# Splitting the left sums of a quad over two pairs and writing ScalarE's order in a fused two-layer graph kernel

## The chip, the cores and the metric

The kernel runs on one core of one Trainium2 chip. A core has TensorE (matrix products into PSUM), VectorE (DVE in the profile), ScalarE (ACT), GpSimd (POOL) and SyncE (SP, which issues transfers), each with an instruction queue of its own, and 16 DMA engines. The metric is the device time of one execution in microseconds; lower is better.

## The reference

There are 128 graphs of 128 nodes with 512 features each, and an adjacency matrix for each graph, all in 32-bit floats. Two residual layers follow each other:

```python
# layer 0
h = maximum(layernorm(x), 0)
Xw = h @ Wv + bv;  sj = Xw @ aw[:d];  si = Xw @ aw[d:]
alpha = adj * exp(leaky_relu(sj[None, :] + si[:, None] + ab, 0.2))
T = alpha / (sum(alpha, -1) + 1e-12)
H = h @ Wk[0] + (T @ h) @ Wk[1] + (T @ T @ h) @ Wk[2] + sum(bk)
x = x + relu(H)
# layer 1
h = maximum(layernorm(x), 0)
q, k = split(h @ Wqk);  v = h @ Wv
w = mask / sqrt(512) * sum(q * (adj @ (k * mask)), -1)
out = x + softmax(w over the nodes) * v
```

## The kernel before

**Tiling.** Two graphs make a pair (64 pairs), two pairs a quad (32 quads). All products of a pair by a weight matrix go through Strassen's scheme: two graphs by two halves of the contraction form a 2x2 block matrix, and seven products on sums of blocks (called 1 to 7) replace eight. The function strassen (L361) writes the products in the order 1, 5, 6, 2, 7, 3, 4 into four PSUM banks a, b, c, e. Between them ScalarE copies partial results from bank to bank or to a buffer: U1, b from a (L378), after product 1; S5, the buffer from e (L380), after product 5; U2, c from b (L382), after product 6; S7, the buffer from c (L386), after product 7. Product 6 adds onto U1, product 7 onto U2, and product 4 adds into c once S7 has read it.

**Layer 0, the loop over pairs (L644).** There are two Strassen rounds in each pass. y10(p) computes h times Wk[1] and Wk[0] in bank set 1 and uses 512 columns; y2(p + 2) computes h times Wk[2] and the attention columns in bank set 2, with 257 columns. One pass p runs, on TensorE: y10(p) with the two transposes of the transition matrix T (t_transposed, L482) after product 2; inner(p) and outer(p), which multiply by the transposed T; y2(p + 2). Around these:
- attention(p) (L453) makes T from the attention columns and the adjacency, on VectorE with one exponential on ScalarE (L463); its last lines multiply the transposed adjacency aT by the mask on ScalarE (L479) and store it for layer 1 (L480).
- outer(p) ends with four drains of the set 1 banks by VectorE (L533), which give the residual x1, and its store.
- seed_a and seed_e (L491, L495) have ScalarE write the bias into banks a and e of set 1 once those are drained; the next y10 adds to it.
- norm2_statistics(p) and norm2(p) (L546, L537) normalise x1 for layer 1: mean and variance on VectorE (L282, L283), a logarithm and an exponential on ScalarE (L287, L288), five small operations on VectorE, two activations over 512 columns on ScalarE (L306). The result is stored in DRAM (h2d) and read back by blocks (hv) for transposing. norm0(p + 3) does the same for the x of a later pair.
- y2's ends: block (0, 0) is copied by ScalarE (Y00, L434) after product 2, block (1, 0) (Y10, L437) after product 4; the other two are VectorE additions.
- prepare (L553) forms weight sums for layer 1 in pairs 3 to 9.

**The left sums of layer 1.** for_layer1(p) (L403), called behind y10(p + 1)'s additions, transposes hv into the tile fw of the pair's quad on VectorE (L412, four transposes of 128x256). The pool of fw has one buffer: `left = layer0.enter_context(tc.tile_pool(name="left", bufs=1))` (L683). In the second pair of a quad, four 128x512 additions and subtractions (L420, L421, L423, L424) complete its eight slots, and two transfers of 1 MB each by GpSimd's queue (L422, L425) store slots 0 to 3 and 4 to 7.

**What sets the order.** The engines run at once; each runs its own instructions in the order in which they stand in its queue. A scheduler decides this order from priorities and dependences. The helper behind (L83) adds to it: an instruction is placed after a named earlier one, `done[what]`. TensorE's order is written out (ordered, L88); on VectorE and ScalarE some places are written and the others are the scheduler's. A new tile in a pool with one buffer is written only when all users of the old tile, transfers among them, are done.

**Layer 1** begins when layer 0's pools are closed (L712). It works quad by quad on the stored sums and doesn't change here.

Of the kernel before, what the change touches and what calls it, by code (L numbers as in the profile page):

```python
# [16 lines left out]
def kernel(  # L17
# [25 lines left out]
    nc = tc.nc  # L43
# [233 lines left out]
    def statistics(src, gate="warm"):  # L277

        mv = small.tile([P, G, 2], FP, name="mv")
        for j in range(G):  # L280
            st = small.tile([P, 6], FP, name="st")
            nc.vector.bn_stats(st, src[:, j, :])  # L282
            nc.vector.bn_aggr(mv[:, j, :], st)  # L283
        mean, var = mv[:, :, 0], mv[:, :, 1]

        r = small.tile([P, 6, G], FP, name="r")
        behind(gate, nc.scalar.activation, r[:, 0], var, AF.Ln, bias=eps)  # L287
        nc.scalar.activation(r[:, 1], r[:, 0], AF.Exp, scale=-0.5)  # L288
        nc.vector.tensor_mul(r[:, 2], r[:, 1], r[:, 1])  # L289
        nc.vector.scalar_tensor_tensor(r[:, 3], var, EPS, r[:, 2], op0=OP.add, op1=OP.mult)  # L290
        nc.vector.tensor_scalar(r[:, 4], r[:, 3], -0.5, 1.5, op0=OP.mult, op1=OP.add)  # L291
        rs = small.tile([P, 2, G], FP, name="rs")
        nc.vector.tensor_mul(rs[:, 0], r[:, 1], r[:, 4])
        done["rs"] = nc.vector.scalar_tensor_tensor(rs[:, 1], mean, -1.0, rs[:, 0], op0=OP.mult, op1=OP.mult).ins  # L294
        return rs

    def norm_relu(src, permuted=False, rs=None):


        rs = statistics(src) if rs is None else rs  # L300
        h = front.tile([P, G, D], FP, name="h")
        for j in range(G):
            to, at = h[:, j, :], src[:, j, :]
            if permuted:
                to, at = unpermuted(to), at.rearrange("p (c f a) -> p c f a", c=DC, f=Q)
            nc.scalar.activation(to, at, AF.Relu, bias=rs[:, 1, j:j + 1], scale=rs[:, 0, j:j + 1])  # L306
        return h

    def unpermuted(h):
# [48 lines left out]
        return dict(zip((5, 6, 7, 3, 1, 2, 4), [s[:, i] for i in range(4)] +  # L358
                        [blocks[0, 0], blocks[0, 1], blocks[1, 1]]))

    def strassen(banks, left, right, s, first, ends, steps={}, gate="warm"):  # L361

        w = right[1].shape[2:]
        a, b, c, e = (t[:, :w[0]] if len(w) == 1 else t for t in banks)

        def product(bank, i, start=False):
            if len(w) > 1:
                bank = bank.rearrange("p (k o) -> p k o", k=w[0])  # L370
            for k in range(HC):
                ordered(nc.tensor.matmul, bank, left[i][:, k * P:(k + 1) * P], right[i][:, k],
                        start=(start and k == 0), stop=(k == HC - 1), skip_group_check=True)
            if i in steps:
                steps[i]()

        product(a, 1, first)
        nc.scalar.copy(b, a)  # L378
        product(e, 5, first)
        done["s"] = behind(gate, nc.scalar.copy, s[:, 0], e).ins  # L380
        product(b, 6)
        done["u2"] = behind("s", nc.scalar.copy, c, b).ins  # L382
        product(a, 2)
        ends[0, 0](a)
        product(c, 7)
        done["s7"] = nc.scalar.copy(s[:, 1], c).ins  # L386
        ends[1, 1](e, s[:, 1])
        product(b, 3)
        ends[0, 1](b, s[:, 0])
        product(c, 4)  # L390
        ends[1, 0](c)
# [6 lines left out]
    def begin(p):  # L398
        hT = lefts.tile([P, G, DC, N], FP, name="x")
        transposed(HV.pop(p), hT)  # L400
        LEFT[p] = left_sums(hT)

    def for_layer1(p):  # L403

        q, second = divmod(p, 2)
        if not second:
            FW[q] = left.tile([P, 8, G, HC, N], FP, name="fw")
        f = FW[q]
        blocks, hv = f[:, L21:SLOT[4] + 1] if second else f[:, 0:SLOT[2] + 1:2], HV2.pop(p)
        for j in range(G):  # L410
            for k in range(2):
                nc.vector.transpose(blocks[:, k, j].rearrange("p f (n b) -> p f n b", n=Q),  # L412
                                    hv[:, j].rearrange("p n (k f a) -> p k f n a", k=2, f=HC)[:, k])
        if second:
            fv = FW.pop(q).rearrange("p o j k n -> p o (j k n)")
            fd = FD[q].rearrange("p o j k n -> p o (j k n)")
            at = {o: fv[:, i] for o, i in SLOT.items()}

            queue = nc.gpsimd if q + 1 < NQ else nc.sync
            nc.vector.tensor_add(at[5], fv[:, L21], at[4])  # L420
            nc.vector.tensor_sub(at[6], at[5], at[1])  # L421
            queue.dma_start(fd[:, :4].rearrange("p o n -> p (o n)"), fv[:, :4].rearrange("p o n -> p (o n)"))  # L422
            nc.vector.tensor_sub(at[7], at[1], fv[:, L21])  # L423
            done["c12"] = nc.vector.tensor_sub(at[3], at[2], at[6]).ins  # L424
            queue.dma_start(fd[:, 4:].rearrange("p o n -> p (o n)"), fv[:, 4:].rearrange("p o n -> p (o n)"))  # L425

    def y2(p, steps={}, gate=None):


        add = partial(behind, gate, nc.vector.tensor_add) if gate else nc.vector.tensor_add  # L430
        y = Y2[p] = front.tile([P, G, 2, WP], FP, name="y2")[:, :, :, :W2]
        s = front.tile([P, 2, WP * 2], FP, name="s", bufs=1)[:, :, :W2]
        strassen(set2, LEFT[p], right2, s, True, {
            (0, 0): lambda a: nc.scalar.copy(y[:, 0, 0], a),  # L434
            (1, 1): lambda e, t: add(y[:, 1, 1], e, t),
            (0, 1): lambda b, t: add(y[:, 0, 1], b, t),
            (1, 0): lambda c: nc.scalar.copy(y[:, 1, 0], c)}, steps)  # L437
        if p > 1:

            t = small.tile([P, G, S32], FP, name="pzt", bufs=1)  # L440
            behind(gate, nc.vector.transpose, t, y[:, :, 0, :S32])
            d = dram.tile([G, Q, S32], FP, name="pzd")
            nc.gpsimd.dma_start(d.rearrange("g q b -> q g b"), t[::S32])  # L443
            PZ[p] = front.tile([P, G, N], FP, name="pz")
            nc.gpsimd.dma_start(PZ[p].rearrange("p g n -> p (g n)"), bcast(d, 0, G * N))
        else:
            PZ[p] = a2[:, :G * N].rearrange("p (g n) -> p g n", g=G)
# [5 lines left out]
    def attention(p, early_work=None):  # L453

        a, y, pz = ag.pop(p), Y2[p], PZ.pop(p)
        z = front.tile([P, G, N], FP, name="z", bufs=1)
        for j in range(G):
            done["pz"] = nc.vector.tensor_scalar(z[:, j, :], pz[:, j, :], y[:, j, 1, HD:], cz,
                                                 op0=OP.add, op1=OP.add).ins
        if early_work:  # L460
            behind("pz", early_work)
        behind("left" if early_work else "pz", nc.vector.scalar_tensor_tensor, z, z, 0.2, z, op0=OP.mult, op1=OP.max)
        done["z"] = nc.scalar.activation(z, z, AF.Exp).ins  # L463
        d = small.tile([P, 2, G], FP, name="d")
        for j in range(G):
            nc.vector.scalar_tensor_tensor(z[:, j, :], z[:, j, :], 1.0, a[:, j, :], op0=OP.mult,
                                           op1=OP.mult, accum_out=d[:, 0, j:j + 1])
        nc.vector.tensor_scalar(d[:, 0], d[:, 0], 1e-12, None, op0=OP.add)
        nc.vector.reciprocal(d[:, 1], d[:, 0])
        t = T[p] = front.tile([P, G, N], FP, name="t", bufs=1)  # L470
        for j in range(G):
            done["t"] = nc.vector.tensor_scalar(t[:, j, :], z[:, j, :], d[:, 1, j:j + 1], None,
                                                op0=OP.mult).ins
        aT = front.tile([P, G, N], FP, name="aT", bufs=1)
        nc.vector.transpose(aT.rearrange("p g n -> p (g n)"),  # L475
                            agb.pop(p).rearrange("p g q i -> p (g q i)"))
        for j in range(G):
            b = p * G + j
            behind("z", nc.scalar.activation, aT[:, j, :], aT[:, j, :], AF.Copy, scale=maskT[:, b:b + 1])  # L479
        nc.sync.dma_start(ATD[p], aT)  # L480

    def t_transposed(p):  # L482
# [54 lines left out]
    def norm2(p):  # L537

        if p not in RS2:
            norm2_statistics(p)  # L540
        rs = RS2.pop(p)
        HV2[p] = by_blocks(behind("s7", norm_relu, X1[p], rs=rs), H2D[p])

    RS2 = {}

# [93 lines left out]
    with tc.issue_after(done["hv"]):  # L639
        load_x(3)  # L640
        load_adj(2)
        rows(rl[:, :, 1], wv1)

    for p in range(NP):  # L644
        def between():
            if p == 0:
# [3 lines left out]
            if p + 2 < NP:  # L650
                behind("t", begin, p + 2)
            if p + 3 < NP:
                behind("left", norm0, p + 3)
            if p == 2:
                rightl.update(behind("rs", combine, {(kh, k): rl[:, kh * HC:(kh + 1) * HC, k]
                                                     for kh in range(2) for k in range(2)},
# [3 lines left out]

        if p > 1:
            behind("rs2", attention, p)
        y10(p, {1: between, 2: lambda: t_transposed(p)})
        if p > 0:
            behind("c12", for_layer1, p - 1)
        if p == NP - 2:
# [19 lines left out]
        if p + 2 < NP:  # L686
            y2(p + 2, {2: partial(norm2_statistics, p)}, "rs2")
        if p + 1 < NP:
            seed_a()
            seed_e()  # L690
        norm2(p)
        if p + 3 < NP:
            load_adj(p + 3)
# [416 lines left out]
```

## Time and profile before

| quantity | value |
|---|---|
| median of 3 runs | 2290.12 us (2287.68 to 2291.49) |
| the profiled execution's own time | 2288.12 us |
| its span, first to last instruction | 2286.3 us |
| TensorE, matmuls | busy 2235.6 us, 98% |
| VectorE / ScalarE / GpSimd | busy 1629.4 / 1273.6 / 700.6 us |
| DMA | 507.78 MB, mean 222 GB/s |
| layer 0 within the span | about 0 to 1480 us; one pair 21.8 to 22.8 us in the steady part |
| PE clock over the span | 0.995 of full speed |

A line of the timeline reads: start and duration in us, engine, source line, operation, output <- inputs, shapes, and in brackets the idle time of the engine before it and what ended it. Line L91 is the helper of all ordered matmuls and L86 that of everything placed by behind, so the tiles tell what an instruction is: `c<-w,x` is product 4 of y2, `c<-t,x` product 4 of y10, or product 7 where it has `sx`. A line of the waits reads: who waited for whom, us in total, times, the longest. The times are of one execution.

### The profile page before, as it was taken

To read this page: it belongs to the slowest core of one execution; us is meant where nothing else is said; L and a number is where in the kernel's file an instruction comes from. 1 tells how busy PE (TensorE), PEld (TensorE's weight loads), DVE (VectorE), ACT (ScalarE), POOL (GpSimd) and SP (SyncE) were. 2 spreads that over 40 slices of the span, in tenths; PEclk is the share of its full clock that TensorE was granted. 3 is DMA by queue.
4 is the path that set the end of the run, shared out by engine and by line. 5 is a ranking of instruction groups with operands and counts; after the bars stand their busy time and mean duration, and the time that the engine had idled before them with its cause. 6 is when DMAs were issued, how large, how long until landed. Compare 5 with 4: busy or idle time off the path is not lost.

```text
span 2286.3 us, 28949 instructions
## 1 busy us (share of the span) xinstructions
PE 2235.6 (98%) x8227; PEld 1544.0 (68%) x8227; DVE 1629.4 (71%) x4463; ACT 1273.6 (56%) x2933; POOL 700.6 (31%) x827
## 2 busy tenths in 40 slices
PE   9899999999999999999999999999999999999998
PEld 5565656566665656666565666578888888888886
DVE  5677767777677677767767776567777776776777
ACT  4455545555555555555555555446666666666665
POOL 3011111221212122121211212145455555455554
PEclk9999999999999999999999999999999999999999
DMA  8587787676766767676676666668888888888877
GB/s 232 162 259 224 238 243 238 199 220 205 225 207 198 239 199 220 206 224 203 202 238 200 217 206 216 200 231 237 234 239 234 238 233 229 247 235 224 254 236 195
DMA packets 343503, 507.78 MB, mean 222 GB/s; under 512 B 33178, under 2 KB 198426, under 8 KB 326958
## 3 DMA queue, kind: packets, MB, share of 16 engines
q1 hardware_dynamic: 302060, 382.40, 52.8%
q0 software_dynamic: 40992, 123.00, 20.2%
q8 instruction: 65, 1.06, 0.2%
q14 instruction: 96, 0.79, 0.1%
q10 hardware_dynamic: 290, 0.53, 0.1%
HBM read 289.62 MB, written 216.18 MB: 221 GB/s over the span
## 4 chain that ended last, share of the span: by engine, by line
PE 77%; ACT 4%; DVE 3%; DMA 2%; issue 1%; POOL 0%; SPq 0%; DVEq 0%; POOLq 0%
PE a L91 23%; PE b L91 21%; PE c L91 21%; PE e L91 13%; ACT h L306 2%; DMA rw<-rwd 1%; DMA h2d<-h 1%; DMA hv<-h2d 0%; ACT b L378 0%; DMA pwd<-pwt 0%; ACT r L288 0%; ACT y L437 0%; DMA pw<-pwd 0%; ACT r L86 0%; DVE r L291 0%
## 5 line engine op out<-in xcount | busy, mean ns | idle before, releaser
L111 POOL DMA_DIRECT2D agb<-in_adj_dram x256 | 150.5, 592 | 524.1 <-DVE aT L475 490.6
L570 POOL TENSOR_TENSOR c<-s,c 128x512 f32<-128x512 f32 (+1 forms) x186 | 199.9, 1089 | 259.6 <-DVE s L570 254.8
L91 PE MATMUL a<-r,x 128*128 128x512 f32 x512 | 241.6, 594 | 4.9 <-ACT a L493 4.8
L91 PE MATMUL b<-rw,in 128*128 128x256 f32 x896 | 216.4, 381 | 0.0
L289 DVE TENSOR_TENSOR r<-r 128x2 f32<-128x2 f32 x128 | 20.6, 161 | 235.4 <-ACT r L288 235.3
L91 PEld LDWEIGHTS b<-rw,in 128*128 128x128 f32 x896 | 171.3, 191 | 23.6
L91 PEld LDWEIGHTS a<-r,x 128*128 128x128 f32 x512 | 97.0, 190 | 101.0 <-issue 92.1
L570 POOL TENSOR_TENSOR c<-c 128x1024 f32<-128x1024 f32 (+1 forms) x70 | 152.4, 2186 | 13.5 <-DVE c L570 13.2
L91 PE MATMUL a<-w,x 128*128 128x257 f32 x512 | 131.9, 380 | 2.0 <-DVE x L338 2.0
L91 PE MATMUL b<-w,sx 128*128 128x257 f32 x512 | 132.1, 380 | 0.3 <-ACT b L378 0.3
L91 PE MATMUL b<-t,sx 128*128 128x512 f32 x256 | 122.2, 599 | 8.3 <-ACT b L378 8.2
L91 PE MATMUL c<-t,x 128*128 128x512 f32 x256 | 121.2, 596 | 4.8 <-ACT s L386 4.8
L378 ACT COPY b<-a 128x257 f32<-128x257 f32 (+1 forms) x128 | 59.4, 464 | 117.6 <-PE a L91 116.0
L443 POOL DMA_DIRECT2D pzd<-pzt x62 | 37.0, 596 | 281.2 <-DVE pzt L86 275.8
L91 PE MATMUL e<-t,sx 128*128 128x512 f32 x256 | 121.3, 596 | 0.0
L306 ACT ACTIVATE h<-xg,rs 128x512 f32<-128x512 f32 x128 | 97.2, 807 | 43.2 <-DVE rs L294 42.2
L91 PE MATMUL c<-t,sx 128*128 128x512 f32 x256 | 120.5, 593 | 0.0
L570 ACT ACTIVATE c<-c,wcol 128x512 f32<-128x512 f32 x125 | 87.1, 719 | 59.7 <-DVE wcol L570 58.7
L91 PE MATMUL b<-r,sx 128*128 128x512 f32 x256 | 120.3, 592 | 0.0
L570 DVE SCALAR_TENSOR_TENSOR junk<-agg,wscale,c 128x512 f32<-128x512 f32 x128 | 97.9, 765 | 31.3 <-POOL c L570 26.0
L422 POOL DMA_DIRECT2D fd<-fw x31 | 17.4, 561 | 310.2 <-DVE fw L421 297.6
L91 PE MATMUL c<-rw,in 128*128 128x256 f32 x448 | 108.5, 382 | 2.8 <-ACT c L570 2.8
(248 smaller groups left out, 5332.4 us busy)
## 6 DMA issues: line engine op xcount, KB each, us to landing
fd<-fw POOLq DMA_DIRECT2D x62, 1024.0 KB, 6.9
x1d<-x SPq DMA_DIRECT2D x64, 512.0 KB, 3.4
h2d<-h SPq DMA_DIRECT2D x64, 512.0 KB, 2.9
hv<-h2d SPq DMA_DIRECT2D x256, 128.0 KB, 4.2
f<-fd SPq DMA_DIRECT2D x32, 1024.0 KB, 6.3
xg<-in_x_dram SPq DMA_DIRECT2D x63, 512.0 KB, 4.6
hd<-h SPq DMA_DIRECT2D x63, 512.0 KB, 2.8
hv<-hd SPq DMA_DIRECT2D x252, 128.0 KB, 3.1
```

What stands on the lines that cost most here:

```text
L91: done["mm"] = op(*args, **how).ins
L111: nc.gpsimd.dma_start(agb[p][c * S32:(c + 1) * S32].rearrange("p g q i -> p (g q) i"), v[c])
L289: nc.vector.tensor_mul(r[:, 2], r[:, 1], r[:, 1])
L306: nc.scalar.activation(to, at, AF.Relu, bias=rs[:, 1, j:j + 1], scale=rs[:, 0, j:j + 1])
L378: nc.scalar.copy(b, a)
L422: queue.dma_start(fd[:, :4].rearrange("p o n -> p (o n)"), fv[:, :4].rearrange("p o n -> p (o n)"))
L443: nc.gpsimd.dma_start(d.rearrange("g q b -> q g b"), t[::S32])
L570: done[engine] = op(*args, **how).ins
```

## The change

Four things change; no product, sum, copy or activation is added or removed, and the same bytes are moved.
- The four left sums of a quad are split: slots 5 and 6 (at[5], at[6]) are formed in the second pair of the quad, as before, and the first half is stored. The other two sums and the second half's store (`upper`) are put off until for_layer1 is called for the first pair of the next quad, just ahead of the request for the new fw tile.
- In y2, Y00 is placed behind the exponential of the second norm's statistics, and S7 behind Y00. The second norm's logarithm stays behind U2.
- The two seeds are placed behind S7 of y2; norm0(p + 3)'s activations behind S7 of y10, while its statistics stay where they were.
- U1 of y10 is placed behind the activations of the second norm, and the mask's multiplications with their store behind U1 (from pair 2 on).

```diff
-        nc.scalar.activation(r[:, 1], r[:, 0], AF.Exp, scale=-0.5)
+        done["ln"] = nc.scalar.activation(r[:, 1], r[:, 0], AF.Exp, scale=-0.5).ins
...
-    def strassen(banks, left, right, s, first, ends, steps={}, gate="warm"):
+    def strassen(banks, left, right, s, first, ends, steps={}, gate="warm", seventh="warm"):
...
-        nc.scalar.copy(b, a)
+        done["ba"] = behind("warm" if first or "h2" not in done else "h2", nc.scalar.copy, b, a).ins
...
-        done["s7"] = nc.scalar.copy(s[:, 1], c).ins
+        done["s7"] = behind(seventh, nc.scalar.copy, s[:, 1], c).ins
...
     def for_layer1(p):
         q, second = divmod(p, 2)
         if not second:
+            if q:
+                SUMS.pop(q - 1)()
             FW[q] = left.tile([P, 8, G, HC, N], FP, name="fw")
...
+            def upper():
+                behind("c12", nc.vector.tensor_sub, at[7], at[1], fv[:, L21])
+                done["c12"] = nc.vector.tensor_sub(at[3], at[2], at[6]).ins
+                store_half(1)
             nc.vector.tensor_add(at[5], fv[:, L21], at[4])
-            nc.vector.tensor_sub(at[6], at[5], at[1])
-            queue.dma_start(fd[:, :4].rearrange("p o n -> p (o n)"), fv[:, :4].rearrange("p o n -> p (o n)"))
-            nc.vector.tensor_sub(at[7], at[1], fv[:, L21])
-            done["c12"] = nc.vector.tensor_sub(at[3], at[2], at[6]).ins
-            queue.dma_start(fd[:, 4:].rearrange("p o n -> p (o n)"), fv[:, 4:].rearrange("p o n -> p (o n)"))
+            done["c12"] = nc.vector.tensor_sub(at[6], at[5], at[1]).ins
+            store_half(0)
+            SUMS[q] = upper
+            if q + 1 == NQ:
+                SUMS.pop(q)()
...
+        def y00(a):
+            done["y00"] = behind("ln" if gate else "warm", nc.scalar.copy, y[:, 0, 0], a).ins
...
-            (0, 0): lambda a: nc.scalar.copy(y[:, 0, 0], a),
+            (0, 0): y00,
...
-            behind("z", nc.scalar.activation, aT[:, j, :], aT[:, j, :], AF.Copy, scale=maskT[:, b:b + 1])
+            behind(gate, nc.scalar.activation, aT[:, j, :], aT[:, j, :], AF.Copy, scale=maskT[:, b:b + 1])
...
             if p + 3 < NP:
-                behind("left", norm0, p + 3)
+                RS0[p + 3] = behind("left", statistics, xg[p + 3])
...
+        def norms():
+            if p and p + 3 < NP:
+                behind("s7", norm0, p + 3, RS0.pop(p + 3))
+        steps = {1: between, 2: lambda: t_transposed(p), 3: norms}
+        if p > 1:
+            steps[5] = lambda: masked(p, "ba")
+        y10(p, steps)
...
-            seed_a()
-            seed_e()
+            behind("s7", seed_a)
+            behind("s7", seed_e)
```

More of the change, by code (lines that the diff above doesn't have):

```diff
@@ L305, in norm_relu @@
                 to, at = unpermuted(to), at.rearrange("p (c f a) -> p c f a", c=DC, f=Q)
-            nc.scalar.activation(to, at, AF.Relu, bias=rs[:, 1, j:j + 1], scale=rs[:, 0, j:j + 1])
+            done["h"] = nc.scalar.activation(to, at, AF.Relu, bias=rs[:, 1, j:j + 1], scale=rs[:, 0, j:j + 1]).ins
         return h
@@ L401, in begin @@
         LEFT[p] = left_sums(hT)
+    SUMS = {}
     def for_layer1(p):
@@ L411, in for_layer1 @@
             for k in range(2):
-                nc.vector.transpose(blocks[:, k, j].rearrange("p f (n b) -> p f n b", n=Q),
-                                    hv[:, j].rearrange("p n (k f a) -> p k f n a", k=2, f=HC)[:, k])
+                done["c12"] = nc.vector.transpose(blocks[:, k, j].rearrange("p f (n b) -> p f n b", n=Q),
+                                                  hv[:, j].rearrange("p n (k f a) -> p k f n a", k=2, f=HC)[:, k]).ins
         if second:
@@ L419, in for_layer1, with store_half @@
             queue = nc.gpsimd if q + 1 < NQ else nc.sync
-            nc.vector.tensor_add(at[5], fv[:, L21], at[4])
-            nc.vector.tensor_sub(at[6], at[5], at[1])
-            queue.dma_start(fd[:, :4].rearrange("p o n -> p (o n)"), fv[:, :4].rearrange("p o n -> p (o n)"))
-            nc.vector.tensor_sub(at[7], at[1], fv[:, L21])
-            done["c12"] = nc.vector.tensor_sub(at[3], at[2], at[6]).ins
-            queue.dma_start(fd[:, 4:].rearrange("p o n -> p (o n)"), fv[:, 4:].rearrange("p o n -> p (o n)"))
+            def store_half(i):
+                half = slice(4 * i, 4 * i + 4)
+                queue.dma_start(fd[:, half].rearrange("p o n -> p (o n)"), fv[:, half].rearrange("p o n -> p (o n)"))
+            def upper():
+                behind("c12", nc.vector.tensor_sub, at[7], at[1], fv[:, L21])
+                done["c12"] = nc.vector.tensor_sub(at[3], at[2], at[6]).ins
+                store_half(1)
+            nc.vector.tensor_add(at[5], fv[:, L21], at[4])
+            done["c12"] = nc.vector.tensor_sub(at[6], at[5], at[1]).ins
[3 more added lines that the diff above has]
+                SUMS.pop(q)()
     def y2(p, steps={}, gate=None):
@@ L432, in y2 @@
         s = front.tile([P, 2, WP * 2], FP, name="s", bufs=1)[:, :, :W2]
+        def y00(a):
+            done["y00"] = behind("ln" if gate else "warm", nc.scalar.copy, y[:, 0, 0], a).ins
         strassen(set2, LEFT[p], right2, s, True, {
-            (0, 0): lambda a: nc.scalar.copy(y[:, 0, 0], a),
+            (0, 0): y00,
             (1, 1): lambda e, t: add(y[:, 1, 1], e, t),
             (0, 1): lambda b, t: add(y[:, 0, 1], b, t),
-            (1, 0): lambda c: nc.scalar.copy(y[:, 1, 0], c)}, steps)
+            (1, 0): lambda c: nc.scalar.copy(y[:, 1, 0], c)}, steps, seventh="y00")
         if p > 1:
@@ L476, in attention, with masked @@
                             agb.pop(p).rearrange("p g q i -> p (g q i)"))
+        MASKED[p] = aT
+        if p < G:
+            masked(p, "z")
+    MASKED = {}
+    def masked(p, gate):
+        aT = MASKED.pop(p)
         for j in range(G):
             b = p * G + j
-            behind("z", nc.scalar.activation, aT[:, j, :], aT[:, j, :], AF.Copy, scale=maskT[:, b:b + 1])
+            behind(gate, nc.scalar.activation, aT[:, j, :], aT[:, j, :], AF.Copy, scale=maskT[:, b:b + 1])
         nc.sync.dma_start(ATD[p], aT)
@@ L541, in norm2 @@
         rs = RS2.pop(p)
-        HV2[p] = by_blocks(behind("s7", norm_relu, X1[p], rs=rs), H2D[p])
+        h = behind("s7", norm_relu, X1[p], rs=rs)
+        done["h2"] = done["h"]
+        HV2[p] = by_blocks(h, H2D[p])
     RS2 = {}
@@ L642 @@
         rows(rl[:, :, 1], wv1)
+    RS0 = {}
     for p in range(NP):
@@ L662 @@
             behind("rs2", attention, p)
-        y10(p, {1: between, 2: lambda: t_transposed(p)})
+        def norms():
[5 more added lines that the diff above has]
+        y10(p, steps)
         if p > 0:
```

## The prediction

> **What bounds the kernel now.** I read the page's busy times first.
>
> ```profile
> span 2286.3 us, 28949 instructions
> PE 2235.6 (98%) x8227; PEld 1544.0 (68%) x8227; DVE 1629.4 (71%) x4463; ACT 1273.6 (56%) x2933; POOL 700.6 (31%) x827
> ```
>
> TensorE is idle for only 2286.3 - 2235.6 = 50.7 us, so nothing done on another engine gains more than that. Next, the waits of PE:
>
> ```profile
> PE b L91 <- ACT b L378: 8.5, 18, 0.6
> PE a L91 <- ACT a L493: 4.8, 2, 3.9
> PE c L91 <- ACT s L386: 4.8, 9, 1.1
> ```
>
> Then the timeline of layer 0. Call "turn k" the stretch from the first product of y2(k+2) to that of y2(k+3), with y10(k+1) in it. From one first inner product (`a<-y,tt`) to the next an undisturbed turn takes 21.758 us (721.60 to 743.35). Summed over the 59 intervals of pairs 3 to 61, the excess over 21.758 is 33.4 us, 21.7 of it in the 49 of pairs 13 to 61. There it repeats every six pairs (1.05, 0.73, 0.74, 0, 0, 0.2): ScalarE's copy of U1 (L378) stands behind two normalisations, or the copy of product 7 (L386) does:
>
> ```profile
> 710.63 1.52 ACT L306 ACTIVATE h<-x,rs 128x512 f32<-128x512 f32 x2 [1.02 <-DVE rs L294]
> ...
> 712.06 0.58 ACT L378 COPY b<-a 128x512 f32<-128x512 f32 x1
> ...
> 712.69 1.98 PE L91 MATMUL b<-t,sx 128*128 128x512 f32 x4 [0.48 <-ACT b L378]
> ```
>
> The copy waits for no product: it starts as the second activation leaves.
>
> **The Trainium skill.** "TensorE: Matmul & The Clock Gate", What's actually happening: TensorE's clock halves after an idle window and recovers after a busy one; the 3413 ns windows run freely. The trace agrees: its three single slow stretches begin at 1461.94, 1530.21 and 2274.31 us, whole multiples of 3.4133 apart. Half a window idle can do, though:
>
> ```profile
> core 0: us, PE busy (x) PEld busy (x) DVE busy (x) ACT busy (x) POOL busy (x), PEclk, DMA share, GB/s
> 1458.53:1461.94 3.41, 1.10 (x3) 0.62 (x4) 3.38 (x8) 1.11 (x2) 1.09 (x2) 1.00 0.46 192
> 1461.94:1465.35 3.41, 3.41 (x6) 1.35 (x5) 1.17 (x7) 0.98 (x3) 0.00 (x0) 0.50 0.98 386
> 1526.80:1530.21 3.41, 1.14 (x5) 1.04 (x6) 3.27 (x8) 3.28 (x13) 0.00 (x0) 1.00 0.91 337
> 59.07:62.48 3.41, 1.43 (x7) 0.93 (x6) 1.45 (x4) 0.00 (x0) 0.00 (x0) 1.00 0.47 114
> 62.48:65.89 3.41, 3.36 (x15) 2.73 (x16) 3.34 (x11) 1.23 (x4) 0.00 (x0) 1.00 0.02 5
> ```
>
> With 1.10 or 1.14 us busy in a window the next ran at 0.50; with 1.43 it did not. So 2.27 us idle inside one window cost half of 3.41 = 1.7 us, 1.98 cost nothing. "DMA: Bandwidth & Descriptors", Anatomy of one DMA: a GpSimd-issued transfer takes about 2.0 us plus its bytes at 436 GB/s, since its semaphore waits for the write receipt: 4.4 us for 1 MB, an estimate; the trace has 5.0 (below) and is used. The same clock page, Architectural detail, says VectorE and ScalarE are strict first-in-first-out; in the trace, too, work stands behind a waiting instruction.
>
> **The change part by part.** Zero is the first y2 product (702.54 in the timeline), undisturbed.
>
> ScalarE's orders (built programs, engine by engine): before, they differ from turn to turn; after, all are U1, S5, U2 of y2, logarithm, exponential, Y00, S7, both seeds, h2, Y10, h2, attention exponential, U1 of y10, mask twice, S5, U2, transposed transition, logarithm and exponential of the next norm (about that copy), S7, h0 twice. No arithmetic is added or removed.
> - U1 (L378): product 1 of y10 (at 6.07) ends near 8.0. In front: S7 4.54, seeds 4.81 and 5.3 (0.59 each), h2 5.75 to 6.5, Y10 to 6.8, h2 to 7.55, exponential to 7.95. U1 goes at 8.0, its limit is near 8.9: the 0.48 us waits go.
> - S7 (L386): before the two h0 of 0.76 each: the 0.46 us waits go. If the logarithm in front were late instead: attention exponential 7.55, its row sums, scaling, transposes, sums and statistics 6.1 us (713.05 to 719.18), logarithm 13.7, exponential to 14.2; S7 is due at 15.1. Covered by 0.9.
> - Second norm's logarithm before Y00 and S7: variance at 2.1, U2 done 3.15, Y00 due 3.67. Covered by 1 us in an ordinary turn.
> - Seeds behind S7 end at 5.9, needed at 6.07 by y10: just covered. Masks and their store (L480) slip by under 1 us; a pair's aT is read only in layer 1.
> - I take 20 of the 33.4 us as recovered; the waits of pairs 3 to 12 for VectorE's e and b and for loads stay in part.
>
> The split of the sums. In odd turns VectorE loses two 128x512 operations, 2 x 0.69 = 1.4 us. In even turns, after the b addition, it has the two upper sums, their 1 MB store by GpSimd, then the next quad's transposes (L412). The buffer has one copy, and in the built program the first transpose waits for the semaphore count that this very store reaches. Before, the store had a whole turn to land. So VectorE stands still for a DMA it has just triggered, and behind it stand the four drains (L533), the statistics and the logarithm, which now stands in ScalarE before Y00 and S7; product 4 of y2, in PE's order, waits for S7. GpSimd's queue: the adjacency chunks and row broadcast ahead of the store are done by about 13.5; the chunk behind it has a turn of slack. SyncE's order inside a turn is unchanged, but its X1 store and load wait with the drains.
>
> ```profile
> L422 POOL DMA_DIRECT2D fd<-fw x31: 542/562/562, 117.7 to 1459.4; - x31
> DMA to landing us min/median/max: 4.3/5.0/7.0
> ```
>
> Median 5.0; the second half behind it can't hold it up much, so I keep 5.0. A late transpose has a precedent in this trace:
>
> ```profile
> 368.52 1.43 DVE L412 STREAM_TRANSPOSE fw<-hv 128x256 f32<-128x256 f32 x4 [3.15 <-DMA hv<-h2d]
> ...
> 369.86 0.39 DVE L533 SCALAR_TENSOR_TENSOR x<-a,xg 128x256 f32<-128x256 f32 x1
> ...
> 372.35 0.30 DVE L283 BATCH_NORM_AGGREGATE mv<-st 128x2 f32<-128x6 f32 x2
> 372.68 0.29 ACT L86 ACTIVATE r<-mv,eps 128x2 f32<-128x2 f32 x1
> 373.01 0.20 ACT L288 ACTIVATE r<-r 128x2 f32<-128x2 f32 x1
> ```
>
> Transpose start F, logarithm F + 4.16, exponential F + 4.49; Y00 0.11 later (728.65, 728.76), S7 0.27 after that, 0.38 long, product 4 0.05 after its end: F + 5.30.
> Now F: e addition 15.77, b 16.85 to 17.55, two sums to 18.93; 0.29 to the issue, 5.0 to landing, 0.12 to VectorE's wake-up (as for L412's other waits): 24.34, that is 2.58 in the next turn. Product 4 at 7.88 instead of 5.21: **2.67 us of PE idle**, with 4.3 and 7.0 us landings 1.97 and 4.67. What follows is shifted alike and catches up: U1 at 10.7 against 11.5 due. The wait falls in k = 2, 4, ..., 60: 30 times. In k = 2 to 8 up to four preparation subtractions (0.7 each, L191 to L194, called from L557) delay the sums by some 1.9 us: about 4.3 us each.
>
> Clock: an idle gap of 2.67 holds 2.1 us of one window in about half of all positions (1.3 + 0.57 of 3.41). Two turns plus 2.67 are 46.2 us, 13.5 windows, so a spared gap is followed by one half a window on, mostly a slow one; with the loss 47.9 us, 14.03 windows, so a hit repeats. I take 20 of 26 at 1.7 us, and 2.5 each for the four long gaps.
>
> Sum: 26 x 2.67 = 69; 4 x 4.3 = 17; clock 34 + 10 = 44; end +6 (in turn 62 the store also stands behind a GpSimd load that waits for y10's last product, and the first layer-1 product for the drain: about 6 us and one slow window, less what the shortened VectorE queue spares of the 3.85 us seed wait); recovered -20. +116 on the profiled execution's own 2288.12 gives 2404; the median shown, 2290.12, is 2 above: **2405**.
>
> **Rivals.**
> 1. The wait bites but the clock stays, as after the 1.98 us idle: +69 + 17 + 7 (long gaps) + 6 - 20 = +79: 2369. For it: 2.67 is near the limit, a 4.3 us landing would give 1.97 (then about 2340).
> 2. Faster: the store lands before VectorE needs the buffer, and the recovered 20 us remain: 2270. It decides at F = -0.09, a landing within 2.3 us of issue; the trace's quickest is 4.3. The same result if the count waited for were an older store's; the program says otherwise.
> 3. Longer: landings near 7, as three or four of 31 have, or gaps covering two windows each: 26 x 4.2 + 26 x 1.7 + 17 + 10 + 6 - 15 = +171: 2460; halfway there, 2435.
> 4. The new order does nothing and split and order cancel: 2290.
>
> **How the numbers follow.** Forecast 0.50, rival 1 0.28, rival 3 0.14, rival 2 0.05, rival 4 0.03. The range 2335 to 2445 takes in rival 1 with its shortest landing and half of rival 3. 0.2% (4.6 us) is about what a measurement can tell from none. Faster 0.05, same 0.02, slower 0.93.
>
> **What would show it.** Right: VectorE idle about 5 us before L416 on a DMA `fd<-fw`, 30 times; PE waiting some 2.7 us for ACT's S7 copy (L386) in every second turn; ordinary turns at 21.76; halved-clock stretches after the gaps; no 0.48 us waits for L378. Wrong: no such idle time on VectorE, or PE's gaps under 1 us because S7 does not stand behind the logarithm; a clock that never drops leaves 2340 to 2370.

## The result and the profile after

The changed kernel takes 2397.51 us (median of 4 runs, 2395.04 to 2402.33) against 2289.59 us (2287.68 to 2291.49) before: 1.0474 times as long, 95% interval 1.0454 to 1.0493. The forecast was 2405. All traces below are of one profiled execution each; that of the changed kernel took 2396.2 us, with a span of 2394.2.

The page after, span and busy times:

```profile
span 2394.2 us, 29193 instructions
PE 2277.6 (95%) x8227; PEld 1568.9 (66%) x8227; DVE 1635.2 (68%) x4463; ACT 1264.6 (53%) x2933; POOL 700.1 (29%) x827
```

TensorE is idle for 116.6 us instead of 50.7, and the same 8227 matmuls are busy 42.0 us longer: part of them ran at a lower clock. Next, the waits of PE (us in total, times, longest):

```profile
PE c L91 <- ACT s L86: 79.0, 32, 6.0
PE a L91 <- issue: 11.8, 1, 11.8
```

The first line is product 4 waiting for the copy S7, now recorded under the helper L86; 31 of the 32 lie in pairs 3 to 61 (74.9 us). The second is the first product of layer 1. Of the waits shown of before, the 9 for L386 are gone, and of the 18 for L378 one is left, 2.0 us in pass 62. The waits of VectorE have a new first line:

```profile
DVE fw L416 <- issue: 174.2, 30, 12.6
```

These are 30 of the 31 first transposes of a later quad. "issue" means that the profile names no releaser for them; the timeline of one such turn, with the store ahead of it, does show what they follow. L426 is the store:

```profile
763.88 0.68 DVE L86 TENSOR_TENSOR fw<-fw 128x512 f32<-128x512 f32 x1
...
764.47 0.69 DVE L430 TENSOR_TENSOR fw<-fw 128x512 f32<-128x512 f32 x1
...
765.46 0.56 POOL L426 DMA_DIRECT2D fd<-fw  x1 [6.47 <-DVE fw L430]
...
770.66 1.43 DVE L416 STREAM_TRANSPOSE fw<-hv 128x256 f32<-128x256 f32 x4 [5.50 <-issue]
...
774.49 0.30 DVE L283 BATCH_NORM_AGGREGATE mv<-st 128x2 f32<-128x6 f32 x2
774.83 0.29 ACT L86 ACTIVATE r<-mv,eps 128x2 f32<-128x2 f32 x1 [3.43 <-DVE mv L283]
775.16 0.20 ACT L288 ACTIVATE r<-r 128x2 f32<-128x2 f32 x1
775.27 0.36 ACT L86 COPY y<-a 128x257 f32<-128x257 f32 x1
...
775.52 0.38 ACT L86 COPY s<-c 128x257 f32<-128x257 f32 x1
...
775.95 1.68 PE L91 MATMUL c<-w,x 128*128 128x257 f32 x4 [2.35 <-ACT s L86]
```

Read down: the two upper sums end at 765.16, the store is issued, VectorE stands 5.50 us, and its transposes start 5.20 us after the issue. Drains, statistics, logarithm, exponential, Y00 and S7 follow without a pause, and product 4 starts 5.29 us after the transposes. The record of all stores of L426, both halves, issue to landing:

```profile
DMA to landing us min/median/max: 4.1/5.1/11.4
```

The late halves alone landed after 5.08 us in the median, and VectorE resumed 0.08 us later. Finally the clock, in windows on the 3.4133 us grid on which the slow stretches start (us, busy time of each engine, PEclk granted, DMA share, GB/s):

```profile
537.47:540.88 3.41, 1.67 (x8) 1.14 (x7) 2.67 (x11) 1.62 (x6) 0.00 (x0) 1.00 0.68 183
540.88:544.29 3.41, 3.41 (x10) 1.71 (x9) 2.70 (x13) 3.41 (x8) 1.72 (x3) 1.00 0.48 151
581.83:585.25 3.42, 2.30 (x11) 1.68 (x9) 3.42 (x11) 0.10 (x1) 0.00 (x0) 1.00 0.37 91
585.25:588.66 3.41, 2.22 (x7) 1.44 (x8) 2.67 (x13) 3.31 (x9) 0.00 (x0) 1.00 0.76 258
772.98:776.39 3.41, 1.06 (x5) 0.60 (x4) 2.67 (x12) 1.53 (x6) 0.00 (x0) 1.00 0.65 205
776.39:779.80 3.41, 3.41 (x7) 1.78 (x6) 2.62 (x12) 2.64 (x5) 1.63 (x3) 0.50 0.36 128
1059.70:1063.12 3.42, 1.54 (x8) 1.02 (x7) 2.68 (x12) 1.94 (x6) 0.00 (x0) 1.00 0.66 208
1063.12:1066.53 3.41, 3.41 (x6) 1.50 (x5) 2.69 (x14) 2.13 (x5) 2.04 (x4) 0.50 0.45 162
```

At 776 the gap of 2.35 us lies wholly inside one window (1.06 busy) and the next runs at 0.50. At 540 the gap was 1.75 us: no loss. At 585 it was 2.31 us, but cut in two by a boundary (2.30 and 2.22 busy): no loss. At 1062 a gap of only 1.88 us, whole in one window (1.54 busy), was followed by a slow one all the same, although 1.67 busy at 540 and the 1.43 shown of before were not; the busy time of a window alone doesn't draw the line in these traces. Besides the gaps at 540 and 585 only the loop's last gap, 1.36 us at 1539, left the clock alone: in pairs 3 to 61 there are 27 slow stretches, 102.4 us or 30 windows.

The difference of the two spans, 107.8 us, splits as follows. The excess is that of the 59 intervals of pairs 3 to 61 over 21.758 us each; slow stretches count half their length.

| term | before | after |
|---|---|---|
| start to the first inner product of pair 3 | 136.24 | 137.29 |
| excess, pairs 3 to 61 | 33.4 | 131.5 |
| of which halved clock | 0 | 51.2 |
| first inner product of pair 62 to the end | 833.0 | 841.6 |

An ordinary pass with the store is 4.23 us over 21.758 (median of those from pair 13 on), the one after it 0.0.

### The profile page after: what moved, and what is told of

Same layout as the page of the kernel before. It is cut to its first block, busy times and chain, and to the rows that moved or that the text cites. A ratio compares the mean times of both kernels' runs of the same rounds, so it can differ in the third digit from the quotient of the medians.

```text
span 2394.2 us, 29193 instructions
## 1 busy us (share of the span) xinstructions
PE 2277.6 (95%) x8227; PEld 1568.9 (66%) x8227; DVE 1635.2 (68%) x4463; ACT 1264.6 (53%) x2933; POOL 700.1 (29%) x827
## 3 DMA queue, kind: packets, MB, share of 16 engines
q8 instruction: 65, 1.06, 0.2%
## 4 chain that ended last, share of the span: by engine, by line
PE 54%; issue 24%; DVE 10%; DMA 5%; POOL 4%; ACT 3%; SPq 0%; POOLq 0%; DVEq 0%; ACTq 0%
PE a L91 17%; PE c L91 14%; PE b L91 13%; PE e L91 9%; POOL agb L111 2%; DVE fw L416 2%; DVE x L559 2%; DMA pzd<-pzt 2%; DVE st L282 2%; POOL pz L462 1%; DVE fw L430 1%; ACT r L86 1%; DMA hv<-hd 1%; DMA pw<-pwd 1%; ACT h L306 0%
## 5 line engine op out<-in xcount | busy, mean ns | idle before, releaser
L91 PE MATMUL a<-r,x 128*128 128x512 f32 x512 | 277.3, 670 | 3.3 <-ACT a L519 3.2
L416 DVE STREAM_TRANSPOSE fw<-hv 128x256 f32<-128x256 f32 x256 | 90.9, 413 | 186.7 <-issue 174.2
L426 POOL DMA_DIRECT2D fd<-fw x62 | 34.7, 559 | 533.1 <-DVE fw L434 306.1
L91 PEld LDWEIGHTS a<-r,x 128*128 128x128 f32 x512 | 112.2, 219 | 116.8 <-issue 106.9
L86 ACT COPY b<-a 128x257 f32<-128x257 f32 (+1 forms) x128 | 59.3, 464 | 189.5 <-PE a L91 186.4
L91 PE MATMUL c<-w,x 128*128 128x257 f32 x256 | 83.9, 458 | 79.0 <-ACT s L86 79.0
L86 ACT ACTIVATE r<-mv,eps 128x2 f32<-128x2 f32 x128 | 38.0, 297 | 157.7 <-DVE mv L283 157.2
L91 PE MATMUL a<-rw,w 128*128 128x256 f32 x448 | 108.6, 383 | 11.8 <-issue 11.8
```

Of the source, the lines that this page charges most:

```text
L86: return op(*args, **how)
L91: done["mm"] = op(*args, **how).ins
L416: done["c12"] = nc.vector.transpose(blocks[:, k, j].rearrange("p f (n b) -> p f n b", n=Q), hv[:, j].rearrange("p n (k f a) -> p k f n a", ...
L426: queue.dma_start(fd[:, half].rearrange("p o n -> p (o n)"), fv[:, half].rearrange("p o n -> p (o n)"))
```

## The experiments

The theory: VectorE waits for a store that the change has put directly ahead of the next quad's transposes, the wait reaches TensorE through logarithm and S7, and the clock adds to it. Rivals: the split itself costs time without the buffer; ScalarE's written order alone is what costs; the wait is hidden when the logarithm no longer stands before S7; the loss is a wait without the clock.

**e1: the split and the order, but two tiles of four slots** instead of one of eight. The late store then holds only the tile of slots 4 to 7; the next quad's first transposes write slots 0 to 3.

```diff
-            FW[q] = left.tile([P, 8, G, HC, N], FP, name="fw")
+            FW[q] = [left.tile([P, 4, G, HC, N], FP, name=f"fw{i}") for i in range(2)]
...
-        blocks, hv = f[:, L21:SLOT[4] + 1] if second else f[:, 0:SLOT[2] + 1:2], HV2.pop(p)
+        blocks, hv = f[1][:, 0:2] if second else f[0][:, 0:SLOT[2] + 1:2], HV2.pop(p)
```

> The changed kernel, with fw made as two tiles of four slots instead of one of eight (same bytes, same orders). The next quad's first transposes then wait only for the lower store, which landed a turn ago. Theory (the buffer's wait carries the whole loss): all steady turns 21.76 us, no halved clock in the loop, time 2260 to 2280 us. Rival (the new ScalarE order, or the store moved into another turn, costs by itself): 2350 us or more.

Measured: 2261.53 us, 0.9875 of before (0.9858 to 0.9893). In its timeline the transposes follow the sums at once:

```profile
748.48 0.68 DVE L430 TENSOR_TENSOR fw<-fw 128x512 f32<-128x512 f32 x1
...
749.19 1.42 DVE L416 STREAM_TRANSPOSE fw<-hv 128x256 f32<-128x256 f32 x4
```

And of its waits of PE for S7 only the one in the first pass is left:

```profile
PE c L91 <- ACT s L86: 4.1, 1, 4.1
```

No slow stretch is left in pairs 3 to 61, and the excess is 1.7 us. The whole loss of the change, and 136 us against the changed kernel, is the wait for this one tile.

**e2: the written order alone**, with the four sums and both stores together as before.

```diff
-            if q:
-                SUMS.pop(q - 1)()
...
-            store_half(0)
-            SUMS[q] = upper
+            queue.dma_start(fd[:, :4].rearrange("p o n -> p (o n)"), fv[:, :4].rearrange("p o n -> p (o n)"))
+            nc.vector.tensor_sub(at[7], at[1], fv[:, L21])
+            done["c12"] = nc.vector.tensor_sub(at[3], at[2], at[6]).ins
+            queue.dma_start(fd[:, 4:].rearrange("p o n -> p (o n)"), fv[:, 4:].rearrange("p o n -> p (o n)"))
```

> The changed kernel with the left sums and both stores back in the quad's second pair, as before; only ScalarE's written order is left. Theory: the 20 us of waits for U1 and S7 go and nothing comes, 2262 to 2282 us. Rival (the logarithm in front of S7 is too early even without the split): 2300 us or more.

Measured: 2258.77 us, 0.9864 (0.9847 to 0.9880), 3 us better than expected. The order is worth 31.6 us by itself (2290.41 before on that chip), and with two tiles the split adds nothing clear to it: e1's interval overlaps this one.

**e3: the split alone**, in the kernel before with the scheduler's order on ScalarE (for_layer1 of the changed kernel, all else as before).

> The kernel before with only the sums split; ScalarE's order is the scheduler's, which here puts the second norm's logarithm behind S7 and the seeds. VectorE should still stand about 5.4 us in every even turn. Theory (the standing VectorE reaches TensorE only through the logarithm in front of S7): 2270 to 2300 us. Rival (the drains and seeds reach TensorE by themselves): 2360 us or more.

Measured: 2344.15 us, 1.0235 (1.0218 to 1.0251), between theory and rival. The expectation that the scheduler's order hides most of the wait failed. In its timeline VectorE stands, no logarithm stands before S7, and product 4 doesn't wait; but the seeds, which follow the drains, come late for y10:

```profile
1068.40 1.42 DVE L416 STREAM_TRANSPOSE fw<-hv 128x256 f32<-128x256 f32 x4 [7.13 <-issue]
1069.75 0.38 DVE L546 SCALAR_TENSOR_TENSOR x<-a,xg 128x256 f32<-128x256 f32 x1
...
1070.16 0.59 ACT L506 COPY a<-bias_a 128x512 f32<-128x512 f32 x1 [2.43 <-DVE x L546]
...
1070.81 1.98 PE L91 MATMUL a<-r,x 128*128 128x512 f32 x4 [1.75 <-ACT a L506]
```

That is one turn. Over the span TensorE waits for the e addition (18.1 us, 25 times), for T (13.8 us, 16), once before the first product of layer 1 (12.1 us) and for the seeds (10.5 us, 6).

**e4: half the late store.** Slots 4 and 5, which are ready, are stored in the second pair; the late store carries 6 and 7, 0.5 MB.

```diff
+            store(slice(4, 6))
...
-                store_half(1)
+                store(slice(6, 8))
```

> The changed kernel with slots 4 and 5 stored a turn earlier, behind the lower half, so that the late store is 0.5 MB instead of 1 MB. Theory: it lands about 1.2 us sooner, PE's gap shrinks from about 2.6 to 1.4 us and is too short for the clock to halve: 2305 to 2330 us. Rival (the landing is mostly a fixed delay, or the clock drops after short gaps too): 2360 to 2397 us.

Measured: 2307.82 us, 1.0073 (1.0051 to 1.0095). The late store landed after 3.35 us instead of 5.08 (medians), VectorE stood 3.72 us instead of 5.44, and a pass with the store was 0.83 us over, not 4.23. The wait follows the size of the transfer; with the gap below 1 us in most passes three slow stretches remain of 27, and the loss against e1 falls from 136 to 46 us.

**e5: filler in the gap.** In those passes six 128x128 products of the identity, 1.5 us in the trace, are put between products 3 and 4 of y2, so that TensorE isn't idle for them. They write spare columns of bank b. Their start flag clears the accumulation state of the bank, and product 6 of the next y2 then overwrites U1 in place of adding to it: the output is off by 0.054 of its size.

```diff
+        for _ in range(filler):
+            ordered(nc.tensor.matmul, banks[1][:, D - P:], ident, ident, start=True, stop=True, skip_group_check=True)
...
-            (1, 0): lambda c: nc.scalar.copy(y[:, 1, 0], c)}, steps, seventh="y00")
+            (1, 0): lambda c: nc.scalar.copy(y[:, 1, 0], c)}, steps, seventh="y00", filler=6 if p > 4 and p % 2 == 1 else 0)
```

> The changed kernel with six unused 128-column products (about 1.3 us, into a part of bank b that nothing reads) between products 3 and 4 of y2 in every odd turn from the third on, thus inside TensorE's gap. The wait for S7 stays as it is. Theory (some 1.9 us of each odd turn is the halved clock, which comes from 2.2 us idle in one window): gaps of about 1.3 us, no halved clock there, 2340 to 2355 us. Rival (the excess is the wait alone): 2397 us or a little more.

Measured: 2355.44 us, 1.0289 (1.0270 to 1.0307), at the upper end of what the theory gave.

**e9: the same filler with start=False**, so that it keeps the bank's state; the values are again those of the changed kernel.

```diff
-            ordered(nc.tensor.matmul, banks[1][:, D - P:], ident, ident, start=True, stop=True, skip_group_check=True)
+            ordered(nc.tensor.matmul, banks[1][:, D - P:], ident, ident, start=False, stop=True, skip_group_check=True)
```

> The kernel of e5 with the fillers' start flag off, so that they add into the unused columns and leave the rest of bank b as it is; in e5 the flag made y2's product 6 overwrite U1 instead of adding to it. Theory: the time is that of e5, 2348 to 2362 us. Rival (the altered values had a part in e5's time): nearer to 2397 us.

Measured: 2360.63 us, 1.0307 (1.0290 to 1.0325): 37 us faster than the changed kernel with more work on TensorE. A pass with the store is 2.55 us over in the median; in the one at 759 TensorE spends 1.50 us on the filler and is idle for 0.96. So the wait itself is about 2.55 us (the 2.35 at 776 is shorter because the recorded times of products overlap: each lasts 1.03 us and the next starts 0.86 later), and the rest of the 4.23 us, 1.68, was the clock: half of 3.4133 us is 1.71. The slow stretches in pairs 3 to 61 fall from 102.4 to 13.7 us.

**e6: the changed kernel with the logarithm behind S7** (statistics requested after product 7, Y00, S7 and U1 free).

```diff
-            done["y00"] = behind("ln" if gate else "warm", nc.scalar.copy, y[:, 0, 0], a).ins
+            done["y00"] = nc.scalar.copy(y[:, 0, 0], a).ins
...
-        RS2[p] = statistics(X1[p], "u2")
+        RS2[p] = statistics(X1[p], "s7")
...
-            y2(p + 2, {2: partial(norm2_statistics, p)}, "rs2")
+            y2(p + 2, {7: partial(norm2_statistics, p)}, "rs2")
```

> The changed kernel with the second norm's logarithm placed behind S7 of y2, and U1 of y10 not behind the norm's activations; the split and its wait stay. Theory: VectorE stands as long as before, but TensorE's gap goes, since the drains and seeds still come in time: 2262 to 2290 us. Rival (the gap moves to the seeds, to U1 or to the next norm): 2320 us or more.

Measured: 2368.75 us, 1.0350 (1.0332 to 1.0367): the rival was right. The waits of PE for S7 are gone and others stand in their place, for the e addition, for T and for the seeds:

```profile
PE e L91 <- DVE e L86: 27.9, 46, 4.2
PE a L91 <- DVE t L489: 19.7, 35, 1.0
PE a L91 <- ACT a L519: 15.3, 10, 4.0
```

Passes without the store are over by 1.30 us too, those with it by 1.79 (medians).

**e7 and e8: e6 and e3 with the two tiles of e1**, to take the buffer's wait out of both.

> The kernel of e6 (logarithm behind S7) with fw as two tiles, so that VectorE no longer stands for the store. It says what of e6's 2369 us is the wait and what the late logarithm. Theory (the wait costs under this order too, only elsewhere: T's transposes, the e addition, the seeds): 2275 to 2300 us. Rival (the late logarithm itself makes VectorE's chain too long): 2330 us or more.

> The kernel of e3 (split alone) with fw as two tiles. Theory (the wait is what made the split slower): 2265 to 2292 us, no slower than before. Rival (moving two sums and a store to the next turn costs under the scheduler's order): 2320 us or more.

Measured: e7 2319.40 us, 1.0128 (1.0113 to 1.0143); e8 2301.88 us, 1.0051 (1.0036 to 1.0066); both between what theory and rival gave. All medians side by side, in us:

| ScalarE's order | sums together | split, one tile | split, two tiles |
|---|---|---|---|
| the scheduler's | 2290 (before) | 2344.2 (e3) | 2301.9 (e8) |
| written, logarithm behind S7 | not run | 2368.8 (e6) | 2319.4 (e7) |
| written as in the change | 2258.8 (e2) | 2397.5 (the change) | 2261.5 (e1) |

Row by row, one tile against two: the wait for the tile costs 42, 49 and 136 us. Two tiles don't bring e7 and e8 down to e1, so a second thing is at work. In e8's timeline, the logarithm that the scheduler put behind U1 of y10:

```profile
1070.95 0.57 ACT L378 COPY b<-a 128x512 f32<-128x512 f32 x1 [1.39 <-PE a L91]
1071.43 0.30 ACT L86 ACTIVATE r<-mv,eps 128x2 f32<-128x2 f32 x1
1071.76 0.20 ACT L288 ACTIVATE r<-r 128x2 f32<-128x2 f32 x1
1072.00 0.16 DVE L289 TENSOR_TENSOR r<-r 128x2 f32<-128x2 f32 x1 [6.51 <-ACT r L288]
```

U1 waits for product 1 of y10, the logarithm stands behind U1, and VectorE stands 6.51 us for its result; attention comes after that on VectorE, and T is late for TensorE (13 waits for it in e8, 14.0 us; 2 before, 1.6 us; none in e1). Over the span VectorE waits here for

```profile
DVE r L289 <- ACT r L288: 308.6, 125, 6.6
```

against 235.3 us before, 339.5 in e7 and 146.1 in e1. The written order, with the logarithm behind U2, is thus a gain as long as the logarithm's data are there. With the late store they aren't, and the same order carries the wait straight to TensorE. What the logarithm's place alone is worth is not shown: e7 differs from e1 also in leaving U1, Y00 and S7 free. The 12.4 us more of waits for T are about the 11 us by which e8 is slower than before; which placement of the scheduler makes T late there was not taken apart.

**e10: e2 with Y00 and S7 free in pairs 0 to 2**, where the first passes still wait for the adjacency and the first norms.

```diff
-            done["y00"] = behind("ln" if gate else "warm", nc.scalar.copy, y[:, 0, 0], a).ins
+            done["y00"] = behind("ln" if p > 2 else "warm", nc.scalar.copy, y[:, 0, 0], a).ins
...
-            (1, 0): lambda c: nc.scalar.copy(y[:, 1, 0], c)}, steps, seventh="y00")
+            (1, 0): lambda c: nc.scalar.copy(y[:, 1, 0], c)}, steps, seventh="y00" if p > 2 else "warm")
```

> The kernel of e2 (order alone) with the new places of Y00 and S7 from y2(3) on, so that in the first turn S7 does not stand behind two norms. Theory: TensorE's 4.1 us wait for S7 in the first turn goes and part of it comes back as the wait for the e addition of the next y10, 2253 to 2258 us. Rival (all of it comes back): 2259 us as e2.

Measured: 2254.35 us (2253.44 to 2255.10), 0.9842 (0.9827 to 0.9857), the lowest median of all, 36 us under before. In the trace the 4.06 us wait for S7 in the first pass is gone, but most of it comes back: the longest wait for the e addition is 4.6 us, against 2.5 in e2. Pair 3's first inner product starts only 0.65 us earlier than in e2 (136.41 against 137.06). That e10 is faster than e2 is not shown: their medians, 4.4 us apart, were taken on different chips, and the intervals of the ratios overlap.

## Why the prediction was right

The forecast held: 2405 said, 2397.5 measured, by the mechanism named. Only the sign asked for on VectorE, a wait put down to a DMA `fd<-fw`, didn't appear as such: the profile names no releaser, and the timeline with e1 and e4 takes its place. Term by term:

- **The wait for the store.** F was put at 2.58 us into the turn; at 770.66, with the first y2 product at 768.24, it was 2.42. The chain from F to product 4 was put at 5.30 us and took 5.29. The gap was put at 2.67 and was 2.55 (e9). e1 shows the cause by removing it, e4 by shrinking it.
- **Number and sum of the waits.** 26 at 2.67 and 4 at 4.3 us made 86 us. With e1's 1.7 us of excess as what remains without the wait, the new loss in pairs 3 to 61 is 131.5 - 1.7 = 129.8 us; less 51.2 for the clock, 78.6 are waits. The four preparation passes were put at 4.3 + 2.5 us each, 27 together; pairs 3 to 9 have 26.7, but one by one they lie between 4.5 and 8.5, so that the close total is partly luck.
- **The clock.** 44 us were forecast and 51.2 came: 30 windows at half speed rather than 26 (24 hits, some of 2.5 us). The argument that two turns, the gap and the loss make 14.03 windows, so that a hit repeats, is what the trace shows (a slow stretch starts on the grid in any case; the 14, again and again, is the evidence): they start at 349.73, 397.52, 445.30 and 493.09 us and from 633.03 to 1493.19 again, 47.79 us or 14.00 windows apart. I had taken 20 of 26 ordinary gaps as hit and 23 were. That a hit needs 2.1 us idle in one window was too strict, since 1.88 us at 1062 was enough. Of the two between 493 and 633 the first was spared with a short gap, the second because the spared loss had moved it onto a boundary.
- **What the order recovers: mis-sized.** I took 20 of 33.4 us, leaving the waits of pairs 3 to 12 in part. e1 has 1.7 us of excess left, so about 32 were recovered, these pairs included. I had looked only at the named copies; the written order also shortens VectorE's waits for the logarithm and exponential (235.3 us before, 146.1 in e1), which I had not counted. How much of the 12 us comes from that is open.
- **The end.** +6 forecast, +8.7 measured. In pass 62 the store took 11.4 us to land, with the DMA engines 97% busy meanwhile, VectorE stood 12.61 us, and the first product of layer 1 waited 11.8 us, longer than the 6 us that I had estimated, with 10.24 us of slow clock at 1581.94 where before had two stretches of 3.41. Part of it was paid back, but not where I had put it: the seed wait only fell from 3.85 to 3.17 us, while of two waits of before in layer 1's first products, 0.94 and 2.66 us, only one of 0.98 is left.
- **The start.** I had nothing for it; it is +1.05. In the first pass S7, now behind the norms, lets product 4 wait 4.06 us, but by e10's trace most of that would otherwise stand before the e addition; the rest of the difference was not taken apart.

So the sum came out near 108 as +98.1 in the loop, +8.7 and +1.05, against +116: the clock and the end cost 10 us more than forecast, the waits 7 less, and the order gave 12 more. These errors partly cancel, so the total is closer than its terms, and that is luck. (2404 and 2 make 2406 and not 2405, which touches nothing.) Rival 1, the wait without the clock, is what e9 comes near to (2360.6, with 1.5 us of filler in each gap); rival 2's arithmetic, 2270 if the buffer is free in time, is e1 at 2261.5, lower by the under-counted recovery. Rival 3 needed landings near 7 us and had 5.08 in the median; rival 4 needed split and order to cancel, and alone they are worth +54 (e3) and -32 us (e2).

The expectations of e3 and e6 were wrong in one and the same step: that VectorE's work still comes in time when VectorE stands 5 us. In both TensorE then waits for the e addition, T and the seeds, so that a logarithm taken out of the way of S7 only moved the wait.

## What to carry to other kernels

When a store is put off to just before the next use of its tile, ask what that tile's next writer waits for: a single-buffered tile is held until the last transfer from it has landed, and cutting it into two tiles, so that the late store holds only its own part, removed the wait at no cost (2397.5 to 2261.5 us). A written order on ScalarE is worth something only while its inputs are on time: the same placement saved 32 us with the sums on time and made the wait three times as dear with them late (136 us against 42 under the scheduler's order). A small gap that recurs with the loop should be held against the clock's windows as well, since here it cost 1.7 us above its own 2.55.

## What was not expected of the hardware

- The gap and the window grid stay in step. A hit lengthens two turns to 14.00 windows, so the next gap falls at nearly the same place in its window, and a sequence of hits ended only when one gap was short (1.75 us at 540, 1.36 at 1539).
- A gap of 2.31 us cost nothing when a boundary cut it, and 2.22 to 2.46 cost 1.7 us each inside one window; 1.88 us at 1062 did too, and 1.75 at 540 did not. In the Trainium skill, "TensorE: Matmul & The Clock Gate", What's actually happening, an idle window is what lowers the clock; here windows that were busy for 1.06 and once for 1.54 of 3.41 us were enough.
- Halving the store to 0.5 MB made it land 1.7 us sooner (5.08 to 3.35).
- The start flag of a product into 128 spare columns changed the later accumulation in other columns of the same bank: the output is off by 0.054 of its size in e5 and right in e9. The Trainium skill, "PSUM — Partial Sum Buffer", The four PSUM rules, says that the flag clears the state of the whole zone and not of the columns written, and the two runs agree.
